# Group norm of the input in steps one image apart beside the first encoding, in text order, and six output tiles in the convolution

## The chip, the cores and the metric

The kernel runs on one core of a Trainium2 chip. A core has five engines with a queue of instructions each: TensorE (matmul, PE in the profile; its weight loads are PEld), VectorE (DVE), ScalarE (ACT), GpSimd (POOL) and SyncE (SP), which here only issues transfers. All share an on-chip memory SBUF of 128 partitions; matmul results land in a second memory, PSUM. Transfers to and from the large memory outside (HBM) are done by 16 DMA engines. Engines run on their own and wait for one another by semaphores. The metric is the device time of one execution in microseconds (us).

## What is computed

The kernel computes two layers over 32 images of 128 channels and 32 x 32 positions, in float32. The change touches the beginning of the first: the group norm of the input, the encoding to 1024 channels, and a causal convolution along the 1024 positions with 64 taps per channel. The reference, cut to this (`_gn`, the head of `_L0_conv_ref`, and what joins them):

```python
def _gn(v, G=32, eps=1e-5):
    g = v.reshape(B_, G, C_ // G, H_, W_)
    m = jnp.mean(g, axis=(2, 3, 4), keepdims=True)
    s = jnp.var(g, axis=(2, 3, 4), keepdims=True)
    return ((g - m) / jnp.sqrt(s + eps)).reshape(v.shape)

# layer 0, on u = _gn(x) as (32, 128, 1024)
h = jnp.einsum('bdl,de->ble', u, W_enc) + b_enc
K = 2.0 * jnp.einsum('dn,dnl->dl', Cc * Bd, vand).real     # 64 taps for each of 1024 channels
z = jnp.swapaxes(h, 1, 2)
y = jnp.fft.irfft(jnp.fft.rfft(z, n=n_fft) * jnp.fft.rfft(K, n=n_fft), n=n_fft)[..., :L]
y = jax.nn.gelu(jnp.swapaxes(y + D[:, None] * z, 1, 2))
g = y @ W_glu + b_glu
g = g[..., :D_MODEL] * jax.nn.sigmoid(g[..., D_MODEL:])
h = _layernorm(h + g, ln_gamma, ln_beta)
out = h @ W_dec + b_dec
# x = x + layer0(_gn(x)); x = x + layer1(_gn(x))   (layer 1: a deformable depthwise convolution, 64 taps)
```

## The kernel before

`ssm_kernel_table` computes the table of taps, mostly on VectorE with some exponentials and sines on ScalarE, and stores it to HBM as kp_d (line 158). `ssm_convolution` then works through the 1024 channels in eight blocks k of 128. For each block, `encode(k)` makes z (two tiles of 64 KiB per partition, z0 and z1, one buffer each) from all 32 images, and `convolve(k, z)` convolves it. `main_block` does all the rest, from 1577.9 us to the end.

**Encoding.** For k > 0, each image is loaded back normalised from u_d (line 214). For k = 0 it is loaded from x (xt, line 217), normalised by `group_norm`, written to u (five buffers), and u is stored to u_d by ScalarE (line 220). `group_norm` needs seven steps: a sum over the positions on ScalarE (164), a 128x1 matmul with gavg that makes the mean over four channels (165), its negative (167), a sum of squares (169), a second small matmul (170), the root (172), and on VectorE the reciprocal (173) and the normalisation (174). Then eight matmuls psz of 128x128 (224; each is two TensorE instructions in the profile, so an image has 16) fill two PSUM tiles, and two VectorE additions put them with the bias into z0 and z1 (231). PSUM has two psz tiles, which the additions free, and three tiles psy, of which the first encoding takes one per image for the two small matmuls.

**Convolution.** A block has 16 groups of eight channels. A group loads a table tile toe from kp_d (252, SP, 768 KB, three buffers), multiplies the rows of z by it (psy, 270), ScalarE copies the overlap (278), VectorE adds it (282), ScalarE applies Gelu into an output tile yo (291), and POOL stores yo to y_d in eight transfers of 128 KB (303). A group has two yo tiles, of 4 KiB per partition each, and the pool `cvy` has four buffers. So Gelu of a group cannot start before the stores of the group two before have landed. POOL's transfers also wait, each for the transfer eight before it. The tiles xt of the first encoding come from the same buffers.

**Order.** The first encoding, with the table, is ordered by a scheduler that moves instructions across one another; from the line `with tc.manual_schedule()` on, each engine takes its instructions as the text issues them. In the order the scheduler chose, seven images are normalised on VectorE between the instructions of the table; later, ScalarE has the root of image b, the squares of b+1, the store of b, then the negative mean and the sum of b+2, and TensorE has psz of b, then the second small matmul of b+1, then the first of b+2.

[...]z1 reuses memory that the table's tiles had, so its first addition waits until kp_d is stored.

Of the kernel before, what the change touches and what calls it, by code (L numbers as in the profile page):

```python
# [7 lines left out]
F32 = mybir.dt.float32  # L8
# [6 lines left out]
P = 128  # L15
B, C, H, W = 32, 128, 32, 32
L = H * W
D = 1024
KD = D // P
# [138 lines left out]
        nc.sync.dma_start(kp_d.rearrange("(k p) o -> p k o", p=P), kp)  # L158


def group_norm(nc, pool, pm, gavg, eps, xt, out):

    s = pool.tile([P, 1], F32, tag="gn_s", name="gn_s")
    nc.scalar.activation(out, xt, AF.Identity, accum_out=s)
    nc.tensor.matmul(pm[:, 0:1], gavg, s, start=True, stop=True)
    nm = pool.tile([P, 1], F32, tag="gn_m", name="gn_m")
    nc.scalar.mul(nm, pm[:, 0:1], -1.0)
    ss = pool.tile([P, 1], F32, tag="gn_ss", name="gn_ss")
    nc.scalar.activation(out, xt, AF.Square, bias=nm, accum_out=ss)
    nc.tensor.matmul(pm[:, 1:2], gavg, ss, start=True, stop=True)  # L170
    r = pool.tile([P, 1], F32, tag="gn_r", name="gn_r")
    nc.scalar.activation(r, pm[:, 1:2], AF.Sqrt, bias=eps)
    nc.vector.reciprocal(r, r)
    nc.vector.tensor_scalar(out, xt, nm, r, op0=ALU.add, op1=ALU.mult)


def ssm_convolution(nc, tc, const, ins, x, u_d, kp_d, y_d):

    ORDER = (0, 2, 1, 3)
    NB = NJ // 2
    RW = TW - P
    QC = 4
    with tc.tile_pool(name="cvt", bufs=3) as tp, tc.tile_pool(  # L190
        name="cvz", bufs=1
    ) as zp, tc.tile_pool(name="cv1", bufs=1) as one, tc.tile_pool(
        name="cvu", bufs=5
    ) as up, tc.tile_pool(name="cvy", bufs=4) as yp, tc.tile_pool(
        name="cvg", bufs=4
    ) as gp, tc.tile_pool(
        name="cv_psz", bufs=2, space=PSUM
    ) as psz, tc.tile_pool(name="cv_psy", bufs=3, space=PSUM) as psy:
        w_enc = one.tile([P, D], F32, tag="w_enc", name="w_enc")
        nc.sync.dma_start(w_enc, ins["W_enc"])  # L200
        b_enc = one.tile([P, D], F32, tag="b_enc", name="b_enc")
        nc.sync.dma_start(b_enc, ins["b_enc_row"].to_broadcast([P, D]))

        def encode(k):

            z = [
                pool.tile([P, P, NB, B], F32, tag=f"z{g}", name=f"z_{k}_{g}")
                for g, pool in enumerate((one, zp))
            ]
            bias = b_enc[:, k * P : (k + 1) * P]  # L210
            for b in range(B):
                u = up.tile([P, L], F32, tag="u", name=f"u_{k}_{b}")
                if k > 0:
                    nc.sync.dma_start(u, u_d[b])
                else:
                    xt = yp.tile([P, L], F32, tag="yo", name=f"xt_{b}")
                    nc.sync.dma_start(xt, x[b])
                    pm = psy.tile([P, 2, 512], F32, tag="ps", name=f"gn_ps_{b}")
                    group_norm(nc, gp, pm[:, 0, :2], const["gavg"], const["eps"], xt, u)
                    nc.scalar.dma_start(u_d[b], u)  # L220
                for g in range(2):
                    ps = psz.tile([P, NB, P], F32, tag="ps", name=f"psz_{k}_{b}_{g}")
                    for j in range(NB):
                        nc.tensor.matmul(  # L224
                            ps[:, j, :],
                            u[:, (NB * g + ORDER[j]) * P : (NB * g + ORDER[j] + 1) * P],
                            w_enc[:, k * P : (k + 1) * P],
                            start=True,
                            stop=True,
                        )  # L230
                    nc.vector.tensor_add(  # L231
                        z[g][:, :, :, b].rearrange("p d j -> p j d"),
                        ps,
                        bias[:, None, :].to_broadcast([P, NB, P]),
                    )
            return z

        def convolve(k, z):
            rows = [t.rearrange("p d j b -> p d (j b)") for t in z]
            waiting = []  # L240

            def finish():
                for work in waiting:
                    work()
                waiting.clear()

            for g in range(P // CG):
                d0 = k * P + g * CG
                toe = tp.tile([P, CG, TW], F32, tag="toe", name=f"toe_{d0}")
                table = kp_d[d0 : d0 + CG, 0:TW]  # L250

                nc.sync.dma_start(
                    toe,
                    bass.AP(
                        tensor=table.tensor,
                        offset=table.offset,
                        ap=[[1, P], [KPW, CG], [1, TW]],
                    ),
                )
                yo = [  # L260
                    yp.tile([P, CG, P], F32, tag="yo", name=f"yo_{d0}_{i}") for i in range(2)
                ]
                for q in range(CG // QC):
                    c0 = q * QC
                    last = None
                    for i in range(2):
                        ps = psy.tile([P, 2, 512], F32, tag="ps", name=f"psy_{d0}_{q}_{i}")
                        ps = ps[:, :, : 2 * TW].rearrange("p h (c n) -> p h c n", c=2)
                        for c in range(QC):
                            nc.tensor.matmul(  # L270
                                ps[:, c // 2, c % 2, :],
                                rows[i][:, g * CG + c0 + c, :],
                                toe[:, c0 + c, :],
                                start=True,
                                stop=True,
                            )
                        over = tp.tile([P, 2, 2, RW], F32, tag=f"t{i}", name=f"t_{d0}_{q}_{i}")
                        nc.scalar.copy(over, ps[:, :, :, :RW])  # L278

                        def carry(to, rows, src):  # L280
                            own = ps[to : to + rows, :, :, P:TW]
                            nc.vector.tensor_add(own, own, src)  # L282

                        carry(64, 64, over[0:64])
                        carry(32, 32, over[64:96])
                        if i > 0:
                            carry(0, 32, last[96:P])
                        finish()

                        def gelu(to=yo[i][:, c0 : c0 + QC, :], ps=ps):  # L290
                            nc.scalar.activation(  # L291
                                to.rearrange("p (h c) l -> p h c l", c=2),
                                ps[:, :, :, RW:TW][:, :, :, ::-1],
                                AF.Gelu_apprx_tanh,
                            )

                        waiting.append(gelu)
                        last = over

                def store(yo=yo, d0=d0):  # L300
                    for i in range(2):
                        for j in range(NB):
                            nc.gpsimd.dma_start(  # L303
                                y_d[d0 : d0 + CG, :, i * NB + ORDER[j], :].rearrange(
                                    "d b l -> b d l"
                                ),
                                yo[i][j * B : (j + 1) * B],
                            )

                waiting.append(store)  # L310
            finish()

        z = encode(0)

        with tc.manual_schedule():
            convolve(0, z)
            for k in range(1, KD):
                convolve(k, encode(k))


def deformable_general(nc, tc, const, ins, x1_d, out, image):
# [7 lines left out]
    with tc.tile_pool(name="gdf1", bufs=1) as one, tc.tile_pool(  # L329
        name="gdf2", bufs=2  # L330
    ) as two, tc.tile_pool(name="gdf3", bufs=3) as three, tc.tile_pool(
        name="gdfw", bufs=4
    ) as wp, tc.tile_pool(name="gdf_dram", bufs=2, space=DRAM) as dram, tc.tile_pool(
        name="gdf_acc", bufs=2, space=PSUM
# [22 lines left out]
        def prepare(b):  # L357

            xt = two.tile([P, L], F32, tag="xt", name=f"gen_dx_{b}")
            nc.sync.dma_start(xt, x1_d[bass.ds(image, 1)].rearrange("o c l -> (o c) l"))  # L360
            v = one.tile([P, L], F32, tag="v", name=f"gen_dv_{b}")
            pm = psum.tile([P, 2], F32, tag="gn_ps", name="gn_ps")
            group_norm(nc, one, pm, const["gavg"], const["eps"], xt, v)

            vT = two.tile([P, NCHUNK, C], F32, tag="vT", name=f"gen_dvT_{b}")
            for g in range(2):
                ps = psum.tile([P, HC, C], F32, tag="tr", name=f"gen_dtr_{b}_{g}")
                for i in range(HC):
                    k = g * HC + i
# [76 lines left out]
        xt, vT, co_d = prepare(0)  # L446
# [837 lines left out]
```

## Time and profile before

| | us |
|---|---|
| median of 3 runs (13683.05 to 13691.02) | 13687.8 |
| the profiled execution | 13693.54 |
| its span in the profile | 13691.8 |
| first psz | 25.9 |
| first psy: start of the first convolution | 199.2 |
| starts of the next seven convolutions | 379.9, 555.1, 731.0, 909.2, 1090.0, 1263.7, 1440.1 |
| last psy | 1536.6 |
| first matmul of the main block | 1577.9 |

Busy times over the span are TensorE 13161.7, VectorE 8807.4, ScalarE 3285.6 and POOL 9028.9 us. Means of the instructions concerned, all from the groups of the trace up to 2100 us:

| line, instruction | count | mean ns |
|---|---|---|
| 164 ScalarE sum | 32 | 1056 |
| 169 ScalarE squares | 32 | 1140 |
| 167 ScalarE negative mean | 32 | 168 |
| 172 ScalarE root | 32 | 260 |
| 173 VectorE reciprocal | 32 | 152 |
| 174 VectorE normalisation | 32 | 810 |
| 231 VectorE z addition | 512 | 1042 |
| 291 ScalarE Gelu | 512 | 603 |
| 303 POOL store, issue | 1024 | 584 |

A store of yo lands 5.0 us (median) after its issue. In a timeline line the columns are start, duration, engine, line, operation, output and inputs, and in brackets the idle time of the engine ahead of it and what ended it. A line of the waits reads: who waited, for what, us in total, times, the longest.

### The profile page before, as it was taken

The numbers are of one execution on the slowest core, as the hardware profiler recorded it, in microseconds if no ns is written. First come the engines' busy times: TensorE is split into PE (matmuls) and PEld (weight loads), VectorE is DVE, ScalarE is ACT, GpSimd is POOL, SyncE is SP. The second block draws the span as 40 slices with busy tenths as digits, with TensorE's granted clock in tenths as the row PEclk, the third lists the DMA queues.
The fourth block names the chain that finished last, engine by engine and source line by source line (L and its number), as shares of the span: only waits on it lengthen the run. The fifth ranks groups of instructions, "written<-read, shape, count | busy, mean of one in ns | idle before, by whom it ended". The sixth has DMA issues, their size and how long they took to land.

```text
span 13691.8 us, 134306 instructions
## 1 busy us (share of the span) xinstructions
PE 13161.7 (96%) x40482; PEld 7261.4 (53%) x40482; DVE 8807.4 (64%) x12719; ACT 3285.6 (24%) x4767; POOL 9028.9 (66%) x8834
## 2 busy tenths in 40 slices
PE   7889899999999999999999999999999999999976
PEld 6888645555555555555555555555555555555533
DVE  6777426666666666666666666666666666666677
ACT  4333222121112222222222121222222222222245
POOL 2444216777777777777777777777777777777766
PEclk8999999999999999999999999999999999999988
DMA  6888518888888888888888888888888888888865
GB/s 222 265 259 264 181 57 222 233 230 229 230 233 234 240 235 234 234 233 229 238 239 233 230 230 231 232 232 241 236 234 236 231 231 235 239 237 229 230 197 166
DMA packets 1715628, 3105.79 MB, mean 227 GB/s; under 512 B 308306, under 2 KB 1018322, under 8 KB 1713874
## 3 DMA queue, kind: packets, MB, share of 16 engines
q1 hardware_dynamic: 1502290, 2641.91, 71.9%
q10 hardware_dynamic: 163456, 320.92, 6.5%
q0 software_dynamic: 49152, 134.28, 3.0%
q8 instruction: 329, 5.39, 0.2%
q14 instruction: 401, 3.28, 0.1%
HBM read 2630.36 MB, written 466.06 MB: 226 GB/s over the span
## 4 chain that ended last, share of the span: by engine, by line
PE 80%; DMA 10%; DVE 4%; ACT 2%; POOL 2%; issue 1%; SPq 1%; ACTq 0%; DVEq 0%; POOLq 0%
PE gpv L752 24%; PE gpg L729 24%; PE dps L1063 23%; DMA ds<-dhat 4%; PE gph L768 3%; DMA y_d<-yo 3%; PE gpo L657 3%; PE psz L224 3%; DVE z L231 2%; PE psy L270 2%; DMA dhat<-dh 1%; DVE ds L1020 1%; POOL y_d L303 1%; ACT ds L1012 1%; DMA dhy<-dhat 1%
## 5 line engine op out<-in xcount | busy, mean ns | idle before, releaser
L1066 DVE TENSOR_TENSOR dp<-dps,k_weight_slots 128x256 f32<-128x256 f32 (+17 forms) x6528 | 3081.4, 482 | 3051.3 <-PE dps L1063 2869.6
L1063 PE MATMUL dps<-ds,dxw 128*128 128x256 f32 (+18 forms) x13056 | 4729.4, 448 | 208.3 <-DVE dp L1066 197.6
L1082 POOL TENSOR_TENSOR dacc<-dacc,dp 128x256 f32<-128x256 f32 (+3 forms) x4736 | 4415.1, 932 | 443.2 <-DVE dp L1077 75.6
L1063 PEld LDWEIGHTS dps<-ds,dxw 128*128 128x128 f32 x13056 | 2472.7, 193 | 3221.1 <-issue 2578.0
L729 PE MATMUL gpg<-gy,g_w_glu 128*128 128x512 f32 x8192 | 3987.7, 593 | 22.5 <-DMA gy<-y_d 15.8
L752 PE MATMUL gpv<-gy,g_w_glu 128*128 128x512 f32 x8192 | 3974.5, 592 | 0.0
L1077 POOL TENSOR_TENSOR dp<-dp 128x512 f32<-128x512 f32 (+3 forms) x2108 | 2621.5, 1244 | 1909.4 <-DVE dp L1066 1906.7
L1020 DVE TENSOR_TENSOR ds<-ds,dhy 128x1024 f32<-128x1024 f32 (+3 forms) x2176 | 3152.6, 1449 | 810.9 <-DMA ds<-dhat 659.2
L729 PEld LDWEIGHTS gpg<-gy,g_w_glu 128*128 128x128 f32 x8192 | 1544.7, 190 | 1238.2 <-issue 966.7
L752 PEld LDWEIGHTS gpv<-gy,g_w_glu 128*128 128x128 f32 x8192 | 1548.7, 189 | 1158.3 <-issue 915.4
L790 POOL TENSOR_TENSOR gs<-gs,gq 128x512 f32<-128x512 f32 x448 | 633.8, 1415 | 1343.7 <-ACT gq L789 1343.7
L789 ACT ACTIVATE gq<-gr 128x512 f32<-128x512 f32 x448 | 282.2, 630 | 4648.5 <-DVE gr L781 4564.7
L303 POOL DMA_DIRECT2D y_d<-yo x1024 | 590.5, 584 | 949.4 <-ACT yo L291 820.9
L736 ACT ACTIVATE gs<-gpg,k_b_glu 128x512 f32<-128x512 f32 x512 | 351.9, 687 | 2490.0 <-PE gpg L729 2355.6
L270 PE MATMUL psy<-toe,z 128*128 128x192 f32 x4096 | 718.3, 335 | 102.0 <-ACT yo L291 100.2
L925 ACT ACTIVATE dh<-dr,k_minus 128x624 f32<-128x624 f32 x768 | 621.7, 810 | 648.3 <-DMA dhat<-dh 569.8
L270 PEld LDWEIGHTS psy<-toe,z 128*128 128x128 f32 x4096 | 675.1, 193 | 144.4 <-ACT yo L291 138.9
L282 DVE TENSOR_TENSOR psy<-psy,t 32x256 f32<-32x256 f32 (+1 forms) x1280 | 554.1, 433 | 272.9 <-ACT t L278 241.1
L760 DVE SCALAR_TENSOR_TENSOR gs<-gpv,k_b_glu,gs 128x512 f32<-128x512 f32 x512 | 379.9, 742 | 437.4 <-PE gpv L752 423.5
L224 PE MATMUL psz<-w_enc,u 128*128 128x128 f32 x4096 | 576.8, 296 | 86.4 <-DVE z L231 40.2
L659 POOL TENSOR_TENSOR gs<-gs,gr 128x512 f32<-128x512 f32 x448 | 634.9, 1417 | 0.0
L926 ACT ACTIVATE dh<-dh,one 128x624 f32<-128x624 f32 x768 | 626.2, 815 | 24.9
(162 smaller groups left out, 6091.4 us busy)
## 6 DMA issues: line engine op xcount, KB each, us to landing
dhy<-dhat SPq DMA_DIRECT2D x1536, 512.0 KB
ds<-dhat SPq DMA_DIRECT2D x1440, 512.0 KB
dhat<-dh ACTq DMA_DIRECT2D x768, 312.0 KB
y_d<-yo POOLq DMA_DIRECT2D x1024, 128.0 KB, 5.0
gy<-y_d SPq DMA_DIRECT2D x512, 256.0 KB
u<-u_d SPq DMA_DIRECT2D x224, 512.0 KB
toe<-kp_d SPq DMA_DIRECT2D x128, 768.0 KB
dxw<-dvt_d SPq DMA_DIRECT2D x1248, 64.0 KB
```

The source lines that it names most:

```text
L224: nc.tensor.matmul(ps[:, j, :], u[:, (NB * g + ORDER[j]) * P : (NB * g + ORDER[j] + 1) * P], w_enc[:, k * P : (k + 1) * P], start=True, st ...
L270: nc.tensor.matmul(ps[:, c // 2, c % 2, :], rows[i][:, g * CG + c0 + c, :], toe[:, c0 + c, :], start=True, stop=True,)
L303: nc.gpsimd.dma_start(y_d[d0 : d0 + CG, :, i * NB + ORDER[j], :].rearrange("d b l -> b d l"), yo[i][j * B : (j + 1) * B],)
L659: nc.gpsimd.tensor_add(sums[0], sums[0], r)
L729: nc.tensor.matmul(gate, w_glu[:, k, D + m * P : D + m * P + P], ys[k], start=(k == 0), stop=(k == KD - 1),)
L752: nc.tensor.matmul(val, w_glu[:, k, m * P : m * P + P], ys[k], start=(k == 0), stop=(k == KD - 1),)
L790: nc.gpsimd.tensor_add(sums[1], sums[1], sq)
L1020: nc.vector.tensor_mul(s[:, :m], s[:, :m], hy[:, :m])
L1063: nc.tensor.matmul(ps, xw[:, j, :], s[:, :m, :, y0 : y0 + ny], start=True, stop=True)
L1066: nc.vector.tensor_mul(prod[:, :m, :, y0 : y0 + ny], ps, w[:, :, :, None].to_broadcast([P, m, KY2, ny]),)
L1077: adder.tensor_add(prod[:, :m, 0], prod[:, :m, 0], prod[:, :m, 1])
L1082: nc.gpsimd.tensor_add(to, to, prod[:, slot : slot + nj, 0])
```

## The change

`group_norm` becomes a generator, `group_norm_steps`, that stops at five points. The first encoding moves into the part in text order and calls the steps of three images by turns, one image apart; the matmuls of an image come three turns after its load. The pool `cvy` gets six buffers instead of four; xt and yo both use it. `deformable_general`, the other user of the group norm, runs the generator through. The other encodings have the same instructions as before.

```diff
-def group_norm(nc, pool, pm, gavg, eps, xt, out):
+def group_norm_steps(nc, pool, pm, gavg, eps, xt, out):
     s = pool.tile([P, 1], F32, tag="gn_s", name="gn_s")
+    nm = pool.tile([P, 1], F32, tag="gn_m", name="gn_m")
+    ss = pool.tile([P, 1], F32, tag="gn_ss", name="gn_ss")
+    r = pool.tile([P, 1], F32, tag="gn_r", name="gn_r")
     nc.scalar.activation(out, xt, AF.Identity, accum_out=s)
+    yield
     nc.tensor.matmul(pm[:, 0:1], gavg, s, start=True, stop=True)
+    yield
     nc.scalar.mul(nm, pm[:, 0:1], -1.0)
     nc.scalar.activation(out, xt, AF.Square, bias=nm, accum_out=ss)
+    yield
     nc.tensor.matmul(pm[:, 1:2], gavg, ss, start=True, stop=True)
+    yield
     nc.scalar.activation(r, pm[:, 1:2], AF.Sqrt, bias=eps)
     nc.vector.reciprocal(r, r)
     nc.vector.tensor_scalar(out, xt, nm, r, op0=ALU.add, op1=ALU.mult)
+    yield
...
-    ) as up, tc.tile_pool(name="cvy", bufs=4) as yp, tc.tile_pool(
+    ) as up, tc.tile_pool(name="cvy", bufs=6) as yp, tc.tile_pool(
...
-            for b in range(B):
-                u = up.tile([P, L], F32, tag="u", name=f"u_{k}_{b}")
-                if k > 0:
-                    nc.sync.dma_start(u, u_d[b])
-                else:
-                    xt = yp.tile([P, L], F32, tag="yo", name=f"xt_{b}")
-                    nc.sync.dma_start(xt, x[b])
-                    pm = psy.tile([P, 2, 512], F32, tag="ps", name=f"gn_ps_{b}")
-                    group_norm(nc, gp, pm[:, 0, :2], const["gavg"], const["eps"], xt, u)
-                    nc.scalar.dma_start(u_d[b], u)
+            def image(b, u):
                 for g in range(2):
...
+            if k > 0:
+                for b in range(B):
+                    u = up.tile([P, L], F32, tag="u", name=f"u_{k}_{b}")
+                    nc.sync.dma_start(u, u_d[b])
+                    image(b, u)
+                return z
+            running = {}
+            def step(b):
+                if b in running:
+                    next(running[b][1])
+            for t in range(B + 3):
+                step(t - 2)
+                if t - 2 in running:
+                    nc.scalar.dma_start(u_d[t - 2], running[t - 2][0])
+                step(t - 1)
+                if t < B:
+                    u = up.tile([P, L], F32, tag="u", name=f"u_{k}_{t}")
+                    xt = yp.tile([P, L], F32, tag="yo", name=f"xt_{t}")
+                    nc.sync.dma_start(xt, x[t])
+                    pm = psy.tile([P, 2, 512], F32, tag="ps", name=f"gn_ps_{t}")
+                    running[t] = u, group_norm_steps(
+                        nc, gp, pm[:, 0, :2], const["gavg"], const["eps"], xt, u
+                    )
+                    step(t)
+                if t >= 3:
+                    image(t - 3, running.pop(t - 3)[0])
+                step(t - 1)
+                step(t)
             return z
...
-        z = encode(0)
         with tc.manual_schedule():
-            convolve(0, z)
-            for k in range(1, KD):
+            for k in range(KD):
                 convolve(k, encode(k))
```

In the built kernel, ScalarE's order per turn is the root of image t-2, its store, the negative mean and the squares of t-1, the sum of t; TensorE's is psz of t-3, the second small matmul of t-1, the first of t; VectorE's is the reciprocal and normalisation of t-2 and the two z additions of t-3. The table's instructions on VectorE stand where they were, with the normalisation of two images and one z addition among them; SP issues the store of kp_d after eight xt loads (nine before) and the first three toe loads after all 32 xt loads (after eleven before). In the convolutions and later encodings each engine has the order it had.

More of the change, by code (lines that the diff above doesn't have):

```diff
@@ L158, in ssm_kernel_table @@
         nc.sync.dma_start(kp_d.rearrange("(k p) o -> p k o", p=P), kp)
-def group_norm(nc, pool, pm, gavg, eps, xt, out):
+def group_norm_steps(nc, pool, pm, gavg, eps, xt, out):
     s = pool.tile([P, 1], F32, tag="gn_s", name="gn_s")
+    nm = pool.tile([P, 1], F32, tag="gn_m", name="gn_m")
+    ss = pool.tile([P, 1], F32, tag="gn_ss", name="gn_ss")
+    r = pool.tile([P, 1], F32, tag="gn_r", name="gn_r")
     nc.scalar.activation(out, xt, AF.Identity, accum_out=s)
+    yield
     nc.tensor.matmul(pm[:, 0:1], gavg, s, start=True, stop=True)
-    nm = pool.tile([P, 1], F32, tag="gn_m", name="gn_m")
+    yield
     nc.scalar.mul(nm, pm[:, 0:1], -1.0)
-    ss = pool.tile([P, 1], F32, tag="gn_ss", name="gn_ss")
     nc.scalar.activation(out, xt, AF.Square, bias=nm, accum_out=ss)
+    yield
     nc.tensor.matmul(pm[:, 1:2], gavg, ss, start=True, stop=True)
-    r = pool.tile([P, 1], F32, tag="gn_r", name="gn_r")
+    yield
     nc.scalar.activation(r, pm[:, 1:2], AF.Sqrt, bias=eps)
@@ L223, in encode @@
                     for j in range(NB):
+                        lo = (NB * g + ORDER[j]) * P
                         nc.tensor.matmul(
[L225 to L229, printed above, removed]
+                            ps[:, j, :], u[:, lo : lo + P], w_enc[:, k * P : (k + 1) * P],
+                            start=True, stop=True,
                         )
@@ L362, in prepare @@
             pm = psum.tile([P, 2], F32, tag="gn_ps", name="gn_ps")
-            group_norm(nc, one, pm, const["gavg"], const["eps"], xt, v)
+            for _ in group_norm_steps(nc, one, pm, const["gavg"], const["eps"], xt, v):
+                pass
             vT = two.tile([P, NCHUNK, C], F32, tag="vT", name=f"gen_dvT_{b}")
```

## The prediction

> **What bounds the kernel now.** I read four views in this order: the chain of work that ended last (page, part 4), the windows of the stages that the diff touches, the list of waits from 0 to 2100 us, and the timeline of a few images of the first encoding.
>
> ```profile
> PE gpv L752 24%; PE gpg L729 24%; PE dps L1063 23%; DMA ds<-dhat 4%; PE gph L768 3%; DMA y_d<-yo 3%; PE gpo L657 3%; PE psz L224 3%; DVE z L231 2%; PE psy L270 2%; DMA dhat<-dh 1%; DVE ds L1020 1%; POOL y_d L303 1%; ACT ds L1012 1%; DMA dhy<-dhat 1%
> ```
>
> Lines 657 to 1063 belong to the main block, which starts at 1577.9 us with line 729 and is not touched. All the change can reach lies ahead of it: y_d<-yo, psz, z, psy, 11% of the span.
>
> ```profile
> core 0: us, PE busy (x) PEld busy (x) DVE busy (x) ACT busy (x) POOL busy (x), PEclk, DMA share, GB/s
> 128.00:150.00 22.00, 15.48 (x80) 15.26 (x80) 12.00 (x17) 10.81 (x26) 0.00 (x0) 0.61 0.54 192
> 1095.00:1184.00 89.00, 77.15 (x451) 72.14 (x449) 61.15 (x142) 49.45 (x113) 63.20 (x110) 1.00 0.92 297
> 1190.00:1264.00 74.00, 68.70 (x512) 61.24 (x511) 65.90 (x67) 1.25 (x3) 5.03 (x9) 1.00 0.74 244
> ```
>
> The first row is the first encoding: no engine is full and TensorE has a clock of 0.61, so a loop of waits sets it. The second is a convolution: DMA is full in practice (0.92 at 297 GB/s). The third is a later encoding: TensorE and VectorE hand PSUM back and forth, and DMA has a quarter to spare.
>
> ```profile
> ACT yo L291 <- DMA y_d<-yo: 113.4, 82, 4.2
> PE psy L270 <- ACT yo L291: 100.2, 80, 3.5
> DVE z L231 <- DMA kp_d<-kp: 6.5, 1, 6.5
> ```
>
> In the eight convolutions ScalarE's Gelu waits 113 us for the stores of the output tile two groups back, and TensorE waits 100 us behind it, 12.5 us per convolution.
>
> ```profile
> 131.87 1.04 DVE L231 TENSOR_TENSOR z<-psz,b_enc 128x512 f32<-128x512 f32 x1 [0.66 <-PE psz L224]
> 132.09 0.26 ACT L172 ACTIVATE gn_r<-gn_ps,eps 128x1 f32<-128x1 f32 x1 [1.80 <-PE gn_ps L170]
> 132.25 1.14 ACT L169 ACTIVATE u<-xt,gn_m 128x1024 f32<-128x1024 f32 x1
> 132.97 0.81 DVE L174 TENSOR_SCALAR u<-xt,gn_m,gn_r 128x1024 f32<-128x1024 f32 x1
> 133.93 3.75 PE L224 MATMUL psz<-w_enc,u 128*128 128x128 f32 x16 [1.45 <-DVE u L174]
> 137.47 0.43 PE L170 MATMUL gn_ps<-gn_ss,gavg 128*128 128x1 f32 x2
> 137.93 0.26 ACT L172 ACTIVATE gn_r<-gn_ps,eps 128x1 f32<-128x1 f32 x1 [1.66 <-PE gn_ps L170]
> ```
>
> This is one turn of the old loop: root, normalisation, the image's 16 psz matmuls, and only then the next image's variance matmul, since it stands behind psz on TensorE. From the psz at 128.78 to the one at 187.86 are 11 turns: 5.37 us each (turns of 4.8 and 5.8). ScalarE waits 1.7 us per turn for a matmul whose input was long ready.
>
> **What the Trainium skill says.** "TensorE: Matmul & The Clock Gate", Part 1 (The HAM clock gate): the array runs at half clock until it has been busy for a window of about 3.4 us. The trace agrees: 16 psz matmuls take 2.57 us in one turn and 3.75 us in another, and the granted clock is 0.61 here against 1.00 in later stages. The same page, "Architectural detail", says ScalarE and VectorE take instructions strictly in order; so a store issued by ScalarE holds up all behind it. The trace shows that (nm at 129.06 follows the store issued at 128.66). "DMA: Bandwidth & Descriptors", "Issuing engines are not separate DMA queues": stores of POOL and loads of SP share 16 engines. The 0.92 above, with y_d stores and toe loads together, agrees. So more tiles can let work wait elsewhere but add no bandwidth.
>
> **Part 1, the first encoding.** The same instructions in another order. Per pass the new order on ScalarE is: root of image t-2, its store, minus-mean and squares of t-1, sum of t. TensorE: psz of t-3, variance matmul of t-1, mean matmul of t. VectorE: reciprocal and normalisation of t-2, both z additions of t-3. psz now works on an image that was normalised a pass earlier, so the old loop is cut. What is late next is ScalarE itself, whose store waits for VectorE. One pass, by gaps seen in the trace: root to reciprocal 0.30 (49.29 to 49.59), to normalisation 0.26 (49.85), to store 0.84 (50.69), to minus-mean 0.40 (128.66 to 129.06), to squares 0.20 (37.67 to 37.87), to sum 1.15, to the next root 1.06. Sum 4.21 us. With TensorE at full clock everything else fits: squares end 3.25 after the root, the variance matmul ends near 3.7, the second z near 3.9. Cold, TensorE needs 3.75 + 0.42 + 0.57 = 4.74 and becomes the bound; with the second z also late for the next reciprocal (z 1.04 each) I get 5.05 at worst. TensorE will be about 70% busy warm, with gaps under 0.8 us where they were 1.45 to 1.8, so it should be warm more often than now; I take 4.45 between 4.21 and 4.78, an estimate.
>
> The start: the z1 tile lies where the kernel table's tiles were and waits for the kp_d store (57.17 us now). The new VectorE order has two images' work between the table's instructions instead of seven. Counting from the second sine (ready 26.9, as now): L146, L76, L145, L147, L148 at 2.2 us each to 38.2, a normalisation 0.8, L154 0.65, one z 1.0, L155 to L157 1.5: the store is issued at about 42.3 instead of 46.9 and, with the 10.25 us that the chain shows for it, frees VectorE at 52.5. Then only two images are normalised instead of seven. The root of image 3 falls at 57.3, that of image 31 28 passes later: 57.3 + 28 x 4.45 = 181.9. Two normalisation-to-z tails (1.4 + two images' z) add 5.9: psy starts at 187.8 instead of 199.2. Gain 11.4; with 4.21 it is 18, with 4.78 2, with 5.05 a loss of 5.
>
> What moves on the queues: 32 stores to u_d stay on ScalarE at 0.35 us of issue each; on SP the first three toe loads go behind all 32 xt loads. The last xt waits for the normalisation of image 25 (about 157 us), toe follows with 30 us in hand: cost nothing. xt has six buffers instead of four, worth the 5 us at most that ScalarE waited for xt, most of it at 45 us, so nothing more.
>
> **Part 2, six output tiles.** Gelu of group g now waits for the stores of group g-3, not g-2. POOL's order is unchanged, and its stores still wait each for the store eight earlier (88.9 us in the waits), so stores don't land sooner; TensorE may be one group, 1 MiB, further ahead when a convolution ends. That 1 MiB moves into the next encoding. Worth per convolution: at least 1.05 MB / 297 GB/s = 3.5 us if DMA never pauses; about 6 us, one group's period under stalls (1108.03, 1114.60, 1120.61, 1126.66), if slack also carries across pauses such as POOL's 3.3 us without data at 1138; never over 12.5. Outside bounds 0 and 10. I take 5. The cover is the encoding's spare DMA: 16.8 MB in 74 us is 227 GB/s; with 3 MiB instead of 2 MiB of backlog it needs 269, under 297, and five u tiles are loaded ahead. Seven convolutions are followed by an encoding: 7 x 5 = 35. The eighth is followed by the weight loads of the main block, which want DMA at once (first matmul 41 us after the last psy), so the backlog is paid there: gain 1 (0 to 5).
>
> **Sum.** 11.4 + 35 + 1 = 47 us. The profiled execution took 13693.5 (span 13691.8 and 1.7 around it): 13646.5. It lies 5.7 above the median 13687.8, which gives 13641.
>
> **Rivals.**
> - DMA already sets the convolution and the stores merely queue (0.92 share speaks for it; POOL idle for want of data at 1138 against it): 1 us each at 7 convolutions, encoding 11, so -19: 13669. Nothing beyond 0.2%, which is about what a measurement of this kernel tells from no change.
> - The slack absorbs nearly all of TensorE's waits (the longest single wait is 3.5 us, below a group of 5.5; against it the DMA share): 8 x 11 + 16 = 104: 13584.
> - On the other side: the backlog starves the u loads at the start of each encoding. Its place is the first 22 us of encodings 1 to 7. If the queues share evenly, u gets 148 GB/s against 227 wanted: 1.7 MB short, against 2.6 MB loaded ahead, which covers it. If only about one u tile is ahead, 1.2 MB is missing, 5 us, and the gain is gone; it decides from 7 us per encoding on. With 11 us and part 1 as forecast: 7 x (11 - 5) - 11 = +31: 13719. No wait of psz for u is in the present list, which speaks against it.
> - The cold clock in part 1 (5.05) with 5 per convolution: -31, 13657, inside the likeliest case's range.
>
> **How the numbers follow.** The likeliest case, -30 to -75, has 0.57; all waits absorbed 0.12; DMA-bound 0.24; starved u 0.07. Faster by over 0.2% (27 us) 0.69, within it 0.24, slower 0.07. Range: from the strong case's 13590 to the edge of the DMA-bound one at 13678.
>
> **What would show it.** Part 1 right: psz in steps near 4.4 us, ScalarE's waits for gn_ps L175 gone and a wait of the u_d store for VectorE in their place, first psy near 188, granted clock above 0.71 (the mean now). Wrong: steps over 5, or the first psy not before 199. Part 2 right: from one first psy to the next 172 us instead of 177.3 (1440.09 - 199.17 over 7), ScalarE's wait for y_d<-yo down from 113 to about 70, POOL busy 5 to 6 us longer into the encodings. Wrong: 177 as before, or psz waiting for u loads. The main block must keep its length, about 12114 us from its first matmul; if that moves, my sum lacks a term.

## The result and the profile after

| | before | after |
|---|---|---|
| median, us (4 runs each, side by side) | 13689.41 (13683.05 to 13695.7) | 13601.33 (13597.15 to 13606.17) |
| the profiled execution, its span | 13693.54, 13691.8 | 13606.17, 13604.5 |
| first psy | 199.2 | 179.6 |
| mean of the seven convolutions k = 0 to 6, first psy to first psz | 103.0 | 93.0 |
| mean of the seven encodings behind them, first psz to first psy | 74.2 | 74.5 |
| first psy of the last convolution to the first matmul of the main block | 137.8 | 136.8 |
| main block, from that matmul to the end of the span | 12113.9 | 12115.1 |

The ratio is 0.9936, with a 95% interval of 0.9919 to 0.9953. The kernel is 88 us faster; 47 were forecast. The span fell by 87.3 us, and the trace says where: 19.6 in the first encoding, 69.9 in the seven convolutions (721.2 to 651.2 in sum), 1.0 behind the last one, less 2.1 given back in the encodings and 1.1 in the main block.

The chain of work that ended last keeps its shape. Of the entries ahead of the main block, the y_d stores and psz are down from 3% to 2% each, psy and z keep 2%, and lines 685 to 1091 are the untouched rest:

```profile
PE gpg L757 24%; PE gpv L780 24%; PE dps L1091 23%; DMA ds<-dhat 5%; PE gph L796 3%; PE gpo L685 3%; PE psy L299 2%; PE psz L223 2%; DMA y_d<-yo 2%; DVE z L227 2%; DVE ds L1048 1%; ACT ds L1040 1%; DMA dhat<-dh 1%; POOL y_d L332 1%; SPq L1029 1%
```

The windows by stage show more. After: a stretch of the first encoding, a convolution from its first to its last matmul with the start of the next psz, and the encoding behind it.

```profile
core 0: us, PE busy (x) PEld busy (x) DVE busy (x) ACT busy (x) POOL busy (x), PEclk, DMA share, GB/s
128.00:150.00 22.00, 17.69 (x111) 16.57 (x109) 15.09 (x21) 12.90 (x30) 0.00 (x0) 0.79 0.70 240
1015.82:1108.66 92.84, 88.56 (x513) 84.10 (x513) 68.55 (x158) 55.47 (x124) 62.88 (x109) 0.98 0.89 291
1108.66:1184.80 76.14, 69.27 (x514) 62.62 (x513) 65.17 (x68) 1.96 (x4) 10.92 (x19) 0.98 0.80 253
```

Before, the whole convolution around the stretch that the prediction read, and the encoding behind it:

```profile
1089.95:1189.52 99.57, 87.50 (x512) 82.46 (x513) 68.57 (x158) 54.88 (x125) 68.25 (x119) 1.00 0.88 283
1189.52:1263.72 74.20, 68.90 (x515) 61.44 (x513) 65.98 (x68) 1.57 (x4) 5.51 (x10) 1.00 0.74 245
```

In the first encoding, TensorE, VectorE and ScalarE are all busier in the same 22 us, which is the same work at a faster turn, and the granted clock is 0.79 where it was 0.61. In the convolution TensorE has the same 512 matmuls, but its idle time fell from 12 us to 4. POOL shows that work moved out of the convolution: 109 to 115 of a convolution's 128 stores are issued within it (118 to 120 before), and here 19 issues fall in the encoding instead of 10. The encoding shown is the one that got longer (76.1); another, from 1278.5 to 1352.7, took 74.2 with 18.

The waits of the stretch from 0 to 2100 us, after:

```profile
POOL y_d L332 <- DMA y_d<-yo: 118.4, 128, 3.5
...
ACT yo L320 <- DMA y_d<-yo: 44.8, 29, 3.8
...
PE psy L299 <- ACT yo L320: 39.8, 31, 3.6
```

ScalarE's wait for the stores fell from 113.4 to 44.8 us and TensorE's wait behind it from 100.2 to 39.8. POOL's own wait, each store for the one eight earlier, rose from 88.9 to 118.4, and that costs nothing here: it is work that waits in POOL's queue while TensorE goes on.

One turn of the first encoding in the timeline, after:

```profile
139.55 0.81 DVE L179 TENSOR_SCALAR u<-xt,gn_m,gn_r 128x1024 f32<-128x1024 f32 x1
...
140.39 0.35 ACTq L250 DMA_DIRECT2D u_d<-u  x1
...
140.79 0.17 ACT L172 ACTIVATE gn_m<-gn_ps 128x1 f32<-128x1 f32 x1 [1.47 <-PE psz L223]
140.99 1.15 ACT L173 ACTIVATE u<-xt,gn_m 128x1024 f32<-128x1024 f32 x1
...
142.14 1.04 ACT L168 ACTIVATE u<-xt 128x1024 f32<-128x1024 f32 x1
...
142.29 0.58 PE L175 MATMUL gn_ps<-gn_ss,gavg 128*128 128x1 f32 x2
...
143.18 0.24 ACT L177 ACTIVATE gn_r<-gn_ps,eps 128x1 f32<-128x1 f32 x1
...
143.65 0.81 DVE L179 TENSOR_SCALAR u<-xt,gn_m,gn_r 128x1024 f32<-128x1024 f32 x1
```

From one normalisation to the next is 4.10 us. The root at 143.18 follows the sum with no wait, because its matmul at 142.29 no longer stands behind psz. The store at 140.39 is issued right behind the normalisation that it waits for, and only then can gn_m (the negative mean) run: ScalarE's 1.47 us of idle time is that wait. The bracket names psz as the releaser, but that is an inference from what ended last; in other turns it names the normalisation.

### The profile page after: what moved, and what is told of

It is laid out like the page before. It is cut to its first block, busy times and chain, and to the rows that moved or that the text cites. A ratio compares the mean times of both kernels' runs of the same rounds, so it can differ in the third digit from the quotient of the medians.

```text
span 13604.5 us, 134029 instructions
## 1 busy us (share of the span) xinstructions
PE 13141.4 (97%) x40482; PEld 7247.4 (53%) x40482; DVE 8821.0 (65%) x12719; ACT 3293.7 (24%) x4767; POOL 9018.9 (66%) x8834
## 4 chain that ended last, share of the span: by engine, by line
PE 82%; DMA 9%; DVE 4%; ACT 2%; POOL 1%; issue 1%; SPq 1%; ACTq 0%; DVEq 0%; POOLq 0%
PE gpg L757 24%; PE gpv L780 24%; PE dps L1091 23%; DMA ds<-dhat 5%; PE gph L796 3%; PE gpo L685 3%; PE psy L299 2%; PE psz L223 2%; DMA y_d<-yo 2%; DVE z L227 2%; DVE ds L1048 1%; ACT ds L1040 1%; DMA dhat<-dh 1%; POOL y_d L332 1%; SPq L1029 1%
## 5 line engine op out<-in xcount | busy, mean ns | idle before, releaser
L299 PE MATMUL psy<-toe,z 128*128 128x192 f32 x4096 | 705.3, 333 | 40.9 <-ACT yo L320 39.8
```

Source lines behind the costliest of these rows:

```text
L299: nc.tensor.matmul(ps[:, c // 2, c % 2, :], rows[i][:, g * CG + c0 + c, :], toe[:, c0 + c, :], start=True, stop=True,)
```

## The experiments

Theories, by the letters of the expectations. For the first encoding: A, the loop through psz is cut because psz works on an image normalised a turn earlier; B, the six xt tiles bring it; C, the distance of psz isn't what counts, and it comes from elsewhere in the new order. For the convolutions: D, the DMA engines set their length, and more output tiles let stores be paid later and fill pauses; E, POOL's chain of stores, each waiting for the one eight earlier, sets it and not the amount of data. F and G are put in the expectations of their runs. Kernels that ran several times have a ratio to the kernel before with its interval; the others ran once, beside the same kernel before (medians 13689.29 in the first set, 13691.64 in the second). The main block, which no edit touches, took 12108 to 12126 us in the nine profiles, so a single total is uncertain by some us, and the stages say more. The edits are against the changed kernel unless said otherwise.

### The new order with four tiles, and the old order with six

```diff
# order_4tiles
-    ) as up, tc.tile_pool(name="cvy", bufs=6) as yp, tc.tile_pool(
+    ) as up, tc.tile_pool(name="cvy", bufs=4) as yp, tc.tile_pool(
# old_6tiles, against the kernel before
-    ) as up, tc.tile_pool(name="cvy", bufs=4) as yp, tc.tile_pool(
+    ) as up, tc.tile_pool(name="cvy", bufs=6) as yp, tc.tile_pool(
```

> The changed kernel with four output tiles instead of six: the new order of the first encoding alone. Theory A (two independent parts: the order sets the first encoding, the tiles the convolutions): first psy near 180 us, convolutions that an encoding follows near 103 us each, in all about 20 us under the kernel before (13669). Rival B (the first encoding is quicker because six xt tiles let the loads run further ahead): first psy back near 199 us and the time of the kernel before (13689).

> The kernel before with six output tiles: the tiles alone. Theory A: first psy near 199 us as before, the seven convolutions near 93 us each instead of 103, in all about 70 us under the kernel before (13619). Rival B: first psy near 180 us as well, 13600. If the two parts need each other, this and the order alone sum to clearly less than the 88 us of both.

| | median, us | ratio (95%) | first psy | mean convolution | mean encoding |
|---|---|---|---|---|---|
| order alone | 13663.17 | 0.9981 (0.9974 to 0.9988) | 178.6 | 101.8 | 74.2 |
| tiles alone | 13632.5 | 0.9959 (0.9945 to 0.9973) | 202.7 | 93.7 | 74.9 |
| both (the change) | 13601.33 | 0.9936 (0.9919 to 0.9953) | 179.6 | 93.0 | 74.5 |

The two parts add up within what these runs can tell: 26 and 57 us, 83 together, against 88 measured for both; the product of the ratios is 0.9940. The order alone moves the first psy by 20.6 us and the tiles alone don't move it forward at all (3.5 us later), so B falls. That the order alone also has convolutions 1.2 us shorter on the mean is not explained. The tiles alone shorten the convolutions, and their waits (0 to 1600 us) show it. Order alone:

```profile
ACT yo L320 <- DMA y_d<-yo: 110.4, 79, 4.8
PE psy L299 <- ACT yo L320: 99.6, 88, 4.6
```

Tiles alone:

```profile
ACT yo L291 <- DMA y_d<-yo: 50.1, 32, 4.5
PE psy L270 <- ACT yo L291: 40.5, 25, 4.3
```

### The loop left closed

psz follows one turn earlier, right behind its image's normalisation, in the same new order otherwise.

```diff
-            for t in range(B + 3):
+            for t in range(B + 2):
...
-                if t >= 3:
-                    image(t - 3, running.pop(t - 3)[0])
+                if t >= 2:
+                    image(t - 2, running.pop(t - 2)[0])
```

> The changed kernel with the matmuls of an image in the same pass as its normalisation, so that they stand ahead of the next image's second small matmul while they wait for the normalisation. Theory A (the gain in the first encoding is that loop's being cut): passes back at 5.0 to 5.5 us instead of about 4.3, first psy at 197 to 207, about 13624. Rival C (the gain is the table being done earlier, since fewer images stand among its instructions): passes stay under 4.6, first psy under 187.

It took 13644.54 us. The turns are 5.36 us, as the kernel before had them (5.37 by the prediction's count), and the first psy falls at 213.5, later than I expected. One turn in its timeline:

```profile
140.84 3.38 PE L223 MATMUL psz<-w_enc,u 128*128 128x128 f32 x16 [1.44 <-DVE u L179]
...
144.06 0.28 PE L175 MATMUL gn_ps<-gn_ss,gavg 128*128 128x1 f32 x2
...
144.37 0.26 ACT L177 ACTIVATE gn_r<-gn_ps,eps 128x1 f32<-128x1 f32 x1 [0.78 <-PE gn_ps L175]
...
145.34 0.81 DVE L179 TENSOR_SCALAR u<-xt,gn_m,gn_r 128x1024 f32<-128x1024 f32 x1
```

The old loop is back: normalisation, psz, the small matmul behind psz, root. With 28 turns, 1.03 us each is 28.8 of the 33.9 us by which the first psy is later than in the changed kernel. So the distance of psz carries the gain of this part, and C falls. It is also 14.3 us later than the kernel before, which has turns as slow but had normalised seven images ahead of the wait for kp_d: without the cut the new order is a loss. Against the old order with six tiles, its first psy is 10.8 us later and its total 12 us higher (13632.5), by this one run.

### Fewer table loads, four tiles

13 of the 16 toe loads of each block are left out: three tables are loaded and used in turn, so most groups are convolved with the wrong taps; instructions on the compute engines are the same.

```diff
-    ) as up, tc.tile_pool(name="cvy", bufs=6) as yp, tc.tile_pool(
+    ) as up, tc.tile_pool(name="cvy", bufs=4) as yp, tc.tile_pool(
...
+            toes = []
...
+                if g < 3:
...
+                    toes.append(toe)
+                toe = toes[g % 3]
```

> New order, four tiles, and only the first three toe tables of each block are loaded, the other thirteen groups use them again (so the convolution works with wrong taps; same instructions on the engines, 10.2 MB less to move per convolution). Theory D (with four tiles the convolution waits because the DMA engines are full): convolutions fall from 103 to 88 to 90 us, Gelu's wait for y_d<-yo to under 20 us in all, about 13570. Rival E (it waits because a store takes its 5 us and POOL issues one only when the eighth before it has landed): convolutions stay over 97 us, over 13625.

It took 13553.43 us, with convolutions of 87.3 us on the mean. One of them, and the waits (0 to 1600 us):

```profile
501.75:589.01 87.26, 87.25 (x512) 82.42 (x513) 68.58 (x158) 56.85 (x125) 68.33 (x119) 1.00 0.75 202
```

```profile
PE psy L303 <- ACT yo L324: 1.3, 2, 1.1
ACT yo L324 <- DMA y_d<-yo: 0.6, 1, 0.6
```

TensorE is busy for the whole window: its own matmuls are all that is left. Four tiles and the same chain of stores on POOL are enough once the loads are gone, and a store of this window lands after 2.9 us (median) where it took 5.0 before. So E falls as a limit of its own, and D stands: the stores are late because they share the DMA engines with the loads. Whether POOL's chain adds to the wait while the loads are there, this run doesn't tell, since it shortened the stores too.

### Half the stores issued by ScalarE, four tiles

```diff
-                            nc.gpsimd.dma_start(
+                            (nc.gpsimd if j % 2 else nc.scalar).dma_start(
```

The pool also has `bufs=4`.

> New order, four tiles, two of the four stores of each tile issued by ScalarE instead of POOL, so that twice as many stores may be under way. Rival E (the wait of each POOL store for the eighth before it lets the DMA engines run dry; 0.91 share and 280 GB/s in the middle of a convolution with four tiles against 0.97 and 311 with six): the middle of the convolutions reaches 0.95 and 305 GB/s and they fall from 102 to 96 us or less. Theory G (what makes the pauses is that Gelu has no free tile, so there is nothing to store): 100 us or more, or longer by ScalarE's issue time, 64 x 0.35 = 22 us per convolution less what is hidden.

A miss: 13820.86 us, and convolutions of 121.3 us. A window of one, and TensorE's wait (0 to 1600 us):

```profile
570.78:690.01 119.23, 95.14 (x513) 87.27 (x514) 68.52 (x158) 54.73 (x125) 34.66 (x60) 0.96 0.79 240
```

```profile
PE psy L299 <- ACT yo L320: 192.9, 109, 3.4
```

The DMA engines moved less in a given time than before (0.79 at 240 GB/s, against 0.88 at 283) and TensorE waited longer. One group of this convolution in the timeline:

```profile
622.95 0.37 ACT L307 COPY t<-psy 128x256 f32<-128x256 f32 x1 [0.65 <-PE psy L299]
...
623.23 3.09 ACTq L332 DMA_DIRECT2D y_d<-yo  x4
...
626.36 0.37 ACT L307 COPY t<-psy 128x256 f32<-128x256 f32 x1 [2.54 <-PE psy L299]
...
627.29 5.69 PE L299 MATMUL psy<-toe,z 128*128 128x192 f32 x32 [1.78 <-ACT yo L320]
...
630.42 0.37 ACT L307 COPY t<-psy 128x256 f32<-128x256 f32 x1 [0.65 <-PE psy L299]
```

Four issues hold ScalarE's queue for 3.1 us, more than twice the 0.35 us each that the expectation reckoned with; the next copy starts only at 626.36, and TensorE, which does 32 matmuls in 5.69 us, waits 1.78 for the Gelu behind it. A group takes 7.47 us (622.95 to 630.42), and sixteen of them 119.5. So the kernel measures a new wait, that of TensorE for a ScalarE that issues, and decides nothing between E and G: why the DMA engines pause with four tiles stays open. The Trainium skill ("DMA: Bandwidth & Descriptors", "Issuing engines are not separate DMA queues") says that issuing from several engines saves issue time alone and adds no bandwidth; as ScalarE's own queue was the brake here, the lower rate doesn't test that.

### Eight output tiles

To fit, u has four tiles instead of five and the overlap tiles two.

```diff
-        name="cvu", bufs=5
-    ) as up, tc.tile_pool(name="cvy", bufs=6) as yp, tc.tile_pool(
+        name="cvu", bufs=4
+    ) as up, tc.tile_pool(name="cvy", bufs=8) as yp, tc.tile_pool(
...
-                        over = tp.tile([P, 2, 2, RW], F32, tag=f"t{i}", name=f"t_{d0}_{q}_{i}")
+                        over = tp.tile([P, 2, 2, RW], F32, tag=f"t{i}", name=f"t_{d0}_{q}_{i}", bufs=2)
```

> The changed kernel with eight output tiles, four u tiles instead of five and two overlap tiles of each kind instead of three, which make room. Theory D (DMA bounds the convolution; each further group of tiles moves 1 MiB of stores, 3.4 us at the 310 GB/s of the middle of a convolution, into the encoding): the seven convolutions fall from 93 to 89 to 90 us (floor 87.1), encodings stay under 76 us, 13575 to 13585. Rival F (the encoding's cover is used up: the backlog now delays the u loads): encodings grow to 78 us or more, total 13595 or worse.

13568.05 us; ratio 0.9909 (0.9892 to 0.9925). The middle of a convolution, the encoding behind it, and that convolution whole:

```profile
1026.43:1062.43 36.00, 35.84 (x213) 33.95 (x212) 29.00 (x68) 23.70 (x53) 26.23 (x47) 1.00 0.98 319
1077.01:1152.94 75.93, 67.64 (x513) 61.03 (x513) 64.75 (x68) 1.96 (x4) 14.41 (x25) 1.00 0.83 265
990.43:1077.01 86.58, 86.42 (x513) 82.34 (x514) 68.51 (x158) 55.63 (x124) 59.31 (x103) 1.00 0.91 299
```

The same mix of loads and stores runs at 0.98 and 319 GB/s for 36 us, so 0.92 at 297 wasn't full. The convolutions reach TensorE's floor (86.9 on the mean), and the rest of the stores, 25 issues, goes into the encoding. There the backlog begins to show, in the waits from 180 to 1577 us:

```profile
PE psz L223 <- DMA u<-u_d: 5.8, 9, 1.0
```

That line does not occur in the changed kernel, and the encodings are 75.6 us on the mean, against 74.5. They stay below F's 78, and the convolutions are better than D's 89 to 90 us, so F doesn't hold, but its wait has appeared. With one u tile fewer as well as more output tiles, I can't say which of the edits makes it.

### Half the table bytes

A tile of the table is a band: only about half of it is not zero. Three standing tiles are zeroed once, and each group loads four strips of 32 partitions and 96 columns, 384 KB instead of 768 KB.

```diff
-                toe = tp.tile([P, CG, TW], F32, tag="toe", name=f"toe_{d0}")
...
+                toe = toes[g % 3]
+                for s in range(4):
+                    lo = P - 32 * (s + 1)
+                    nc.sync.dma_start(
+                        toe[32 * s : 32 * s + 32, :, lo : lo + 96],
+                        bass.AP(
+                            tensor=kp_d.tensor,
+                            offset=kp_d[d0 : d0 + CG, 0:TW].offset + 32 * s + lo,
+                            ap=[[1, 32], [KPW, CG], [1, 96]],
+                        ),
+                    )
...
+            toes = [
+                one.tile([P, CG, TW], F32, tag=f"toe{i}", name=f"toe_{i}") for i in range(3)
+            ]
+            for toe in toes:
+                nc.gpsimd.memset(toe, 0.0)
```

> The changed kernel with three standing toe tiles that are zeroed once; per group only the 96 columns in which each strip of 32 partitions can have taps are loaded (four transfers of 96 KB instead of one of 768 KB). Theory D: half of the toe bytes gone, 22 MB per convolution to move, so with six tiles TensorE's floor of 87.1 us sets the convolution (88 at most), 13602 - 7 x 5.5 - 2 = 13561. If small rows cost as much as large ones (384 bytes instead of 768, as many packets), convolutions stay near 93 us and 13600.

13543.87 us; ratio to the kernel before 0.9891 (0.9874 to 0.9907). This is the best kernel of the study, 148 us under the kernel before in the same set of runs. A convolution and the encoding behind it:

```profile
981.93:1068.31 86.38, 86.38 (x512) 82.39 (x513) 68.50 (x158) 56.33 (x125) 65.58 (x114) 1.00 0.87 254
1068.31:1142.49 74.18, 68.37 (x515) 61.30 (x513) 65.46 (x68) 1.52 (x4) 8.09 (x14) 1.00 0.78 244
```

TensorE never waits in the convolution, and only 14 issues are left for the encoding, which keeps its 74.2 us. With the bytes halved instead of postponed, the same floor is reached with six tiles and without the eight-tile kernel's longer encodings. The total is 17 us better than expected: from the first psy of the last convolution to the main block it is 127.7 us, 10 less than before, which I had not counted, and the main block itself took 5.7 us less, for which I have no reason.

## Why the prediction came out as it did

**Right in kind, in both parts.** Each part gains, in the place and by the wait that was named: ScalarE's wait for gn_ps fell (gn_r behind the variance matmul from 33.5 us to 2.6 between 60 and 178 us) and the store's wait for VectorE came in its place; ScalarE's Gelu waits less for stores (44.8 us for 113.4). The sum, 47 us, was too small by about 40, and the 88 us lie outside the 30 to 75 of the likeliest case, so the direction and the waits were right and both sizes were not.

**First encoding: 11.4 forecast, 19.6 measured.** The issue of kp_d was forecast at 42.3 and came at 42.11. The turn was taken at 4.45, between 4.21 warm and 5.05 cold at worst; the mean over 28 turns is 4.33 (the normalisations from 52.44 to 173.79). They come in two lengths, mostly three of 4.10 and one of 5.03. TensorE's gaps, forecast under 0.8 us, are 0.46 to 0.77 with one of 1.58 between 139 and 157 us. The granted clock rose to 0.78 (57 to 179.6 us) from 0.71, but that is a mean of two states: in the eight turns from 131.35 to 165.87 us it goes 1.00, 1.00, 0.63, 0.62 and again 1.00, 1.00, 0.60, 0.64. It falls after two turns in which TensorE is busy for 1.9 and 2.7 of 4.1 us and returns after two in which it is busy for 3.6 of 4.1 and for all of 5.0; the first slow turn still fits into 4.10 us. That agrees in kind with the Trainium skill ("TensorE: Matmul & The Clock Gate", Part 1), by which the array is slow until it has been busy for a window; what share of busy time suffices isn't to be read from this case. The prediction's "warm more often" holds, but its shorter gaps did not keep the array warm. Over 28 turns that is 3.3 us better than forecast. The larger error is the term "10.25 us that the chain shows" for the store of kp_d. It is the duration of this store beside the traffic of the old order, carried over to another moment. After:

```profile
42.11 0.39 SPq L158 DMA_DIRECT2D kp_d<-kp  x1
...
47.27 1.02 DVE L227 TENSOR_TENSOR z<-psz,b_enc 128x512 f32<-128x512 f32 x1 [5.23 <-DMA kp_d<-kp]
```

Before:

```profile
46.90 0.39 SPq L158 DMA_DIRECT2D kp_d<-kp  x1
...
57.17 1.90 DVE L231 TENSOR_TENSOR z<-psz,b_enc 128x512 f32<-128x512 f32 x2 [6.51 <-DMA kp_d<-kp]
```

From issue to the first z addition are 5.2 us instead of 10.3. VectorE is free at 47.3 us, not 52.5, and the root of image 3, forecast at 57.3, is at 51.96, 5.3 us earlier. 5.3 and 3.3, less 0.4 for a longer end (6.3 us from the last root to psy for 5.9), make the 8.2 us between 187.8 and 179.6. Beside the store the engines had other transfers before: in its 10.3 us they moved 3.96 MB at a full share, in the 5.2 us after 1.61 MB, of which 1.3 are the store. Two other kernels with the new order (order alone, loop left closed) have 5.2 us too, the old order with six tiles 11.5. That the traffic beside it makes the difference fits all five, and no run changes this traffic alone. The 4.21 that "gaps seen in the trace" gave for a warm turn was 0.11 too long.

**Convolutions: 5 each forecast, 10.0 measured.** This term was mis-sized, at the outer end of the bounds 0 to 10 that the prediction had set. Its base was "DMA is full in practice (0.92 at 297 GB/s)", from which followed 3.5 us for one group's stores moved into the encoding and 1.5 for pauses. The 3.5 was good: mean rate times length is 274.1 GB/s x 103.02 us = 28.24 MB per convolution before and 291.7 x 93.03 = 27.14 after, 1.1 MB less, one group's stores (1.05 MB), or 3.8 us at the new rate. The pauses were undersized: the same 28.24 MB at 291.7 instead of 274.1 GB/s is 6.2 us shorter. About 4 of these are pauses (the share of the whole convolution rose from 0.865 to 0.896, so the engines stand for 9.7 us instead of 13.9); the rest is that they moved more per busy time, for which no run gives the reason. The window that gave 297 GB/s left out the ends of the convolution, and it was one convolution, the shortest of the seven. The mean of seven, by distance from the first psy (DMA share, GB/s):

| us from the first psy | before | changed | eight tiles |
|---|---|---|---|
| 12 to 24 | 0.94, 292 | 0.94, 295 | 0.95, 294 |
| 24 to 36 | 0.91, 282 | 0.96, 311 | 0.97, 308 |
| 36 to 48 | 0.89, 274 | 0.97, 306 | 0.99, 318 |
| 48 to 60 | 0.91, 276 | 0.97, 317 | 0.98, 315 |
| 60 to 72 | 0.93, 293 | 0.96, 302 | 0.99, 318 |
| 72 to 84 | 0.90, 274 | 0.96, 327 | 0.99, 353 |

With four tiles the engines pause for 6 to 11% of each slice; with a group more in hand there are 3 to 6% of pauses. That POOL soon has nothing to store when Gelu stands still would explain it, and isn't shown.

TensorE tells the same gain in another way. Over all eight convolutions its wait for Gelu fell by 60 us (100.2 to 39.8), and its matmuls were also busy for 13 us less (718.3 to 705.3), which makes about the 74 us by which the eight became shorter. The second part goes with the granted clock: before, two convolutions at a mean of 0.95 have TensorE busy for 92 us and two at 1.00 for 88. The prediction counted the waits alone.

So the rival that gave DMA-bound convolutions 1 us each took the right limit and the wrong capacity, and the prediction's base of 297 GB/s shared that error. The rival in which slack absorbs nearly all of the waits had 11 us per convolution and 16 for the encoding; the measured 10.0 and 19.6 are its numbers almost, but not by its reasoning: 39.8 us of TensorE's 100.2 us of waits are left, and part of the gain is the higher rate.

**Smaller steps.** The last convolution with the way to the main block gained 1.0, as forecast, and for the reason given: it is itself 4.1 us shorter (96.9 to 92.7), and the pause before the main block is 3.1 longer (41.0 to 44.1). That the figure fits so well is luck, since two other kernels with six tiles have 134.5 and 133.9 here for the 136.8 of this one. The starved u loads did not come: there is no wait of psz for u in the changed kernel. The encodings are longer by 2.1 us in sum over seven, all but 0.2 of it in the one of 76.1 us, where psz waits for the z additions. One more tile pair, in the eight-tile kernel, shows that wait for the first time. From one first psy to the next the forecast was 172 us, and it is 167.6 (93.03 + 74.55). ScalarE's wait was forecast at about 70 and is 44.8; POOL's extra issues in the encodings, forecast as 5 to 6 us, are about 8 stores of 0.58 us, 5 us. The main block kept its length within 1.1 us.

## What to carry to other kernels

A high mean DMA share isn't proof of a full DMA: look at it by slice, and if it pauses while an engine waits for a free buffer, one more buffer can gain pauses as well as the bytes that it postpones. A transfer's duration belongs to the traffic beside it (a y_d store took 5.0 us beside the table loads and 2.9 without) and isn't carried over to an order that changes that traffic. And where a small operation closes a loop through a long one on the same in-order engine, issue the long one a turn later, but count what start the old order had: the same reordering without the cut came to its first psy 14 us later than the kernel before.

## What the runs showed of the hardware that was not expected

- Much the same mix of table loads and output stores ran at 0.92 and 297 GB/s with four output tiles (1095 to 1184 us) and at 0.98 and 319 GB/s with eight (36 us in the middle of a convolution).
- Halving the table's bytes with rows of 384 bytes instead of 768 did not halve their time, and still paid. In the convolutions shown, SyncE's queue used 32.8% of the engines' time for 7.55 MB with the strips, 3.8 us per MB, and 45.8% for 12.85 MB with the whole tiles, 3.3 us per MB. The Trainium skill ("DMA: Bandwidth & Descriptors", Specifications) puts the line rate at 512 bytes and up, which agrees as far as it goes. But the stores beside the strips also took longer, 3.3 us per MB for 2.8, so what the short rows alone cost isn't shown.
- The share of busy time and the rate need not go together: without most of the table loads the engines were busy for 0.75 of the time and moved 202 GB/s, 269 for a full share, where with them it is 322 (0.88 at 283).
- A transfer's issue isn't free to the engine that makes it: four stores in a row held ScalarE's queue for 3.1 us, and with half of the y_d stores there a convolution took 121.3 us on the mean instead of 101.8.
